# The first and third difference of W_v: a negation, an adding transfer and another order of subtraction

## The chip, the core and the metric

One core of a Trainium2 chip runs the kernel. TensorE multiplies into PSUM, VectorE (DVE), ScalarE (ACT) and GpSimd (POOL) work on SBUF, the first two of them on PSUM as well, and SyncE (SP), ScalarE and GpSimd issue transfers. The metric is the time of one execution in microseconds on the device, as the median of several runs.

## What is computed

A layer of masked attention over 2708 nodes of 1024 features, with a normalised input and a residual:

```python
h = relu(layernorm(x))
q = h @ W_q.T + b_q; k = h @ W_k.T + b_k; v = h @ W_v.T + b_v
z = (q @ k.T) / sqrt(1024) * adj
z = where(z == 0, -10000, z)
out = x + relu(softmax(z, axis=1) @ v)
```

`adj` is 2708 x 2708 with about 4 ones in a row (each is one with probability 0.0014771). Everything is float32.

## The kernel before

**Algebra.** The scores need only M = W_q^T W_k, formed once; then q = h M per tile of 128 nodes, and a score is the dot product of a node's row of q with a neighbour's row of h. The sums of neighbours are taken over rows of h, and W_v is applied to those sums. So the large products are h M ("q" units) and u W_v ("o" units), u being the weighted sums.

**Units.** A unit is two tiles against a 1024 x 1024 matrix B. It is done with seven block products of 512 x 512 instead of eight. B is needed as blocks B11, B21, B22 and as four differences: T0 = B12 - B11, T1 = B22 - T0, T2 = B22 - B12, T3 = B21 - T1. They live in two SBUF tensors: `M[:, i, j]` holds block Bij (8 KB a partition each), `T[:, 0..3]` the differences (`T` is a view of the tensor `wlow`). Ten q units (n = 0 to 9, B = M) are followed by ten o units (n = 10 to 19, B = W_v) and one single tile. `last_q` is 9. Block `M[:, 0, 1]`, B12, enters no product: it is used only to form T0 and T2.

**A unit's products, in TensorE's order** (`multiply`): s2 T1 into bank Y, a12 B21 into X, s4 B22 into Z, s3 T2 into Y; then, for the next unit already (`opened`), a11 B11 into its X, a ScalarE copy of X as its Y (`psy`, line 1024), s1 T0 into its Z, a copy of that as `p5` (line 1027); and last a22 T3 into this unit's Y. Between s3 T2 and a22 T3 the bank Y is read: in the last q units by VectorE's add of line 1092, in earlier or later ones through a ScalarE copy (`taken`, line 1076).

**Blocks of W_v** replace those of M as the last q unit finishes with each place. Lines 1263 to 1266 issue the five loads on SP's queue: B12 at step (n - last_q, i) = (-1, 0), the others at (0, 0) to (0, 4), and lines 1267 to 1270 the four subtractions on VectorE, 128 x 2048 elements each. `i` counts the places in a unit where other work is slipped in (`after(i)`).

**Gathers.** A neighbour's rows come by indirect transfers of 512 KB that GpSimd issues (line 610) into slots of 4 KB a partition; VectorE reads a slot for a score (line 863, with the tile's q rows, `pq`) and again for the weighted sum (line 923), then the slot is free for the next gather. There are 11 slots, and after step (1, 1) two more, cut from `M[:, 0, 1]`. Each transfer of GpSimd's queue also waits for the one eight places ahead of it to land.

**What sets the order.** VectorE's order is written by hand in the text of the program. From unit 4 on those of ScalarE, GpSimd, TensorE and SP are made by the scheduler of the language, which places an instruction when it expects its inputs to be ready; so a load or a ScalarE step may stand units ahead of the place where the text issues it.

Of the kernel before, what the change touches and what calls it, by code (L numbers as in the profile page):

```python
# [14 lines left out]
AF = mybir.ActivationFunctionType  # L15
ALU = mybir.AluOpType
# [49 lines left out]
def tile_preln_masked_attention(  # L66
# [12 lines left out]
    nc = tc.nc  # L79
# [3 lines left out]
    scale = 1.0 / math.sqrt(D)  # L83
# [116 lines left out]
    M = core.tile([P, 2, 2, 4, NB], FT, name="M")  # L200
# [232 lines left out]
    T = wlow.rearrange("p (k a) (b w) -> p k (a b) w", a=2, b=2)  # L433
# [12 lines left out]
    with tc.tile_pool(name="w", bufs=1, side="left") as wp:  # L446
# [11 lines left out]
        t1 = [work.tile([P, D], FT, tag="hT", name=f"t1_{k}", bufs=2) for k in range(2)]  # L458
# [61 lines left out]
        if True:  # L520
# [13 lines left out]
            for o in range(DC):  # L534
# [4 lines left out]
                else:  # L539
                    k = o - H  # L540
# [18 lines left out]
        Z = [psum.tile([P, NB], FT, tag="acc", name=f"ps_z{i}") for i in range(H)]  # L559
# [44 lines left out]
    def small(name):  # L604
        return half.tile([P, NB], FT, tag="half", name=name, bufs=14)
# [183 lines left out]
    slots, free = [], []  # L789
# [219 lines left out]
    def add_block(bank, a, b, last=True):  # L1009
        for c in range(4):  # L1010
            mm = nc.tensor.matmul(bank, a[:, c, :], b[:, c, :], start=False, stop=(c == 3), skip_group_check=True)  # L1011
        return mm
# [3 lines left out]
    def opened(n):  # L1016

        if n not in banks_of:
            return
        X, Z = banks_of[n]  # L1020
        ops = ops_of[n][0]
        add_block(X, ops["a11"], M[:, 0, 0])
        Y = psum.tile([P, NB], FT, tag="acc", name="psy")
        nc.scalar.copy(Y, X)
        products.append(add_block(Z, ops["s1"], T[:, 0]))
        p5 = small("p5")
        nc.scalar.copy(p5, Z)
        opened_of[n] = Y, p5

    def between(n):  # L1030

        if n == len(units) - 1:
            single["first"] = one_started(single["banks"], single["turned"][:, 0:4, :])
        else:
            opened(n + 1)
# [9 lines left out]
    def multiply(n, results, after):  # L1045


        X, Z = banks_of.pop(n)
        ops = ops_of.pop(n)[0]
        Y, p5 = opened_of.pop(n)  # L1050
        after(0)
        after(1)
        products.append(add_block(Y, ops["s2"], T[:, 1]))
        u2 = small("u2")
        nc.scalar.copy(u2, Y)
        after(2)
        add_block(X, ops["a12"], M[:, 1, 0])
        results[0](X)
        after(3)
        products.append(add_block(Z, ops["s4"], M[:, 1, 1]))  # L1060
        results[2](Z, u2)
        after(4)
        products.append(add_block(Y, ops["s3"], T[:, 2]))
        results[1](Y, p5)
        after(5)
        between(n)
        add_block(Y, ops["a22"], T[:, 3])
        results[3](Y)
        after(6)
# [117 lines left out]
    def of_wv(i, j):  # L1187

        return wv[j][:, i * 4:(i + 1) * 4, :]
# [5 lines left out]
    units = [("q",) + p for p in q_pairs] + [("o",) + p for p in o_pairs]  # L1195
# [19 lines left out]
    products = []  # L1215
    last_q = len(q_pairs) - 1
# [10 lines left out]
    single = {}  # L1227

    opened(0)
    for n, unit in enumerate(units):  # L1230
        kind, ta, tb = unit
# [12 lines left out]
        def after(i):  # L1244
# [13 lines left out]
            if n == FIRST and i in (1, 4, 5):  # L1258
                for g in slots[:4] if i == 1 else slots[4:6] if i == 4 else slots[6:8]:
                    with tc.issue_after(sorted_at[-1].ins):  # L1260
                        nc.vector.memset(g, 0.0)
            b11, b12, b21, b22 = M[:, 0, 0], M[:, 0, 1], M[:, 1, 0], M[:, 1, 1]
            for at, place, src in (((-1, 0), b12, of_wv(0, 1)), ((0, 0), b11, of_wv(0, 0)), ((0, 2), T[:, 1], of_wv(1, 1)),
                                   ((0, 3), b21, of_wv(1, 0)), ((0, 4), b22, of_wv(1, 1))):
                if (n - last_q, i) == at:
                    nc.sync.dma_start(place, src)
            for at, place, a, b in (((0, 2), T[:, 0], b12, b11), ((0, 4), T[:, 1], T[:, 1], T[:, 0]),
                                    ((1, 0), T[:, 2], b22, b12), ((1, 1), T[:, 3], b21, T[:, 1])):
                if (n - last_q, i) == at:
                    nc.vector.tensor_sub(place, a, b)  # L1270
            if (n - last_q, i) == (1, 1):
                free.extend(M.rearrange("p i j (a c) w -> p i j a (c w)", a=2)[:, 0, 1, a, :] for a in range(2))
            if (n, i) == (FIRST, 5):
                next(stream)
            if (n, i) == (FIRST, 6):
# [39 lines left out]
            if nxt is None and i == 1:  # L1315
                uT = work.tile([P, D], FT, tag="hT", name="T_alone", bufs=2).rearrange("p (c q) -> p c q", q=P)
# [53 lines left out]
    y = work.tile([P, D], FT, tag="q", name="y_alone", bufs=4)  # L1370
    send(gather(y, x, alone, SLOTS, P))
    uT, (X, Z), p1 = single["turned"], single["banks"], single["first"]
    add_block(Z, uT[:, 0:4, :], T[:, 0])
    add_block(Z, uT[:, 4:8, :], M[:, 1, 1])
    nc.vector.tensor_add(p1, Z, p1)
    nc.vector.scalar_tensor_tensor(y[:, hi], p1, 0.0, y[:, hi], op0=ALU.max, op1=ALU.add)
# [9 lines left out]
    with tc.If(some > 0):  # L1386
# [19 lines left out]
        with tc.tile_pool(name="big", bufs=1, side="right") as big, tc.tile_pool(  # L1406
# [25 lines left out]
            for t, (t0, n) in enumerate(tiles):  # L1432
                ht = gen.tile([P, D], FT, tag="ht", name="g_h")
                nc.sync.dma_start(ht[:n], h_dram[t0:t0 + n, :])
                for s in range(DC // 4):
                    pt = psum.tile([P, 4, P], FT, tag="tp", name="g_pt")
                    for c in range(4):
                        k = s * 4 + c
                        nc.tensor.transpose(pt[:, c, :n], ht[:n, k * P:(k + 1) * P], ident[:n, :n])
                    nc.vector.tensor_copy(hT[:, s * 4:(s + 1) * 4, t0:t0 + n], pt[:, :, :n])  # L1440
            with tc.For_i(0, NT) as i:
# [9 lines left out]
                q = gen.tile([P, D + 1], FT, tag="q", name="g_q")  # L1451
# [25 lines left out]
                for b0 in range(0, N, NB):  # L1477
                    w = min(NB, N - b0)
# [84 lines left out]
```

## Time and profile before

| | us |
|---|---|
| three runs | 639.73, 642.82, 648.21 |
| median | 642.82 |
| the profiled execution | 638.0 |
| its span, first to last instruction | 636.3 |

TensorE's granted clock is 0.995 in the mean. Busy shares by engine: PE 98%, DVE 83%, POOL 57%, ACT 45%; the DMA engines moved 180.11 MB, a mean of 283 GB/s. A timeline row reads: start, duration, engine, line, operation, output<-inputs, shape, count, and in brackets the idle time before it and what ended that. The rows of a group in the list of lines end with busy time, mean ns of one, and idle time before. For indirect transfers a row of POOL is the issue, not the transfer; the line "DMA to landing" has the times from issue to the last byte.

### The profile page before, as it was taken

The page shows a single profiled execution, that of the slowest core. Times are in us where ns is not written, and L with a number is a line of the kernel's source. Part 1 is how long each engine was busy: PE and PEld are TensorE (multiplying, and loading weights), DVE is VectorE, ACT ScalarE, POOL GpSimd, SP SyncE. Part 2 cuts the span into 40 slices and gives each one's busy share as a digit, 9 for nine tenths or more (in the row PEclk, how much of TensorE's full clock was granted, in tenths as well). Part 3 has the DMA queues.
Part 4 walks back from the last instruction along what each step waited for, and adds up shares of the span by engine and source line. Part 5 has one row for each costly group of instructions (what it writes and reads, how often), then busy time and mean ns, then how long its engine had stood idle before and what let it go on. Part 6 is the DMA issues. An engine that isn't in the chain of part 4 may idle for free.

```text
span 636.3 us, 6139 instructions
## 1 busy us (share of the span) xinstructions
PE 624.6 (98%) x1627; PEld 315.5 (50%) x1627; DVE 525.7 (83%) x1021; ACT 283.5 (45%) x421; POOL 361.8 (57%) x383
## 2 busy tenths in 40 slices
PE   9999999999999999999999999999999999999994
PEld 5777766444444544444444434444444444444441
DVE  5999889897995755997889999999999989898341
ACT  3539975859667533424341243443343333422300
POOL 2649960975868277563742563576566777632431
PEclk9999999999999999999999999999999999999997
DMA  8998897598696439986699998999999999893761
GB/s 339 407 372 310 334 351 298 199 342 328 246 382 221 170 113 334 326 299 196 194 289 323 297 412 216 311 318 324 351 378 321 334 299 295 242 289 95 210 217 40
DMA packets 62352, 180.11 MB, mean 283 GB/s; under 512 B 10039, under 2 KB 17031, under 8 KB 61672
## 3 DMA queue, kind: packets, MB, share of 16 engines
q0 software_dynamic: 25136, 78.41, 39.4%
q1 hardware_dynamic: 31242, 80.19, 35.8%
q10 hardware_dynamic: 5934, 21.06, 8.5%
q8 instruction: 15, 0.25, 0.2%
q14 instruction: 25, 0.20, 0.1%
HBM read 147.23 MB, written 42.31 MB: 298 GB/s over the span
## 4 chain that ended last, share of the span: by engine, by line
PE 85%; DVE 6%; issue 4%; DMA 3%; SPq 1%; POOL 0%; ACT 0%; POOLq 0%; DVEq 0%; ACTq 0%
PE ps L1011 38%; PE psy L1011 28%; PE ps_y L476 6%; PE ps_x L476 4%; PE ps_z L476 4%; PE pt L415 3%; DVE u L923 2%; DMA g<-h_dram,tab 1%; DMA or<-u_dram 1%; DVE junk L863 1%; DVE s L722 1%; DVE wlow L1270 1%; PE ps_y L511 1%; SPq L700 1%; DVE q L1092 0%
## 5 line engine op out<-in xcount | busy, mean ns | idle before, releaser
L610 POOL DMA_INDIRECT g<-h_dram,tab x94 | 121.4, 1291 | 84.4 <-DVE u L923 31.1
L1011 PE MATMUL ps<-M,a 128*128 128x512 f32 x320 | 144.0, 593 | 0.0
L1011 PE MATMUL psy<-wlow,s 128*128 128x512 f32 x320 | 143.9, 592 | 0.0
L863 DVE SCALAR_TENSOR_TENSOR junk<-g,pq 128x1024 uint8<-128x1024 f32 x93 | 113.7, 1222 | 14.0 <-DMA g<-h_dram,tab 10.9
L1011 PEld LDWEIGHTS ps<-M,a 128*128 128x128 f32 x320 | 59.8, 190 | 70.8 <-issue 70.6
L1011 PEld LDWEIGHTS psy<-wlow,s 128*128 128x128 f32 x320 | 59.7, 190 | 70.2 <-issue 69.4
L923 DVE SCALAR_TENSOR_TENSOR u<-g,coef,u 128x1024 f32<-128x1024 f32 x69 | 88.4, 1281 | 6.9 <-ACT u L912 5.8
L389 DVE FIND_INDEX8 at<-ones,adj 128x8 uint32<-128x685 f32 (+1 forms) x88 | 74.5, 865 | 0.0
L1011 PE MATMUL psy<-wlow,a 128*128 128x512 f32 x160 | 72.0, 593 | 1.4 <-DVE q L1092 1.4
L1011 PE MATMUL ps<-M,s 128*128 128x512 f32 x160 | 72.1, 592 | 0.0
L1011 PE MATMUL ps<-wlow,s 128*128 128x512 f32 x160 | 72.0, 593 | 0.1
L368 ACT ACTIVATE sized<-adj 128x2708 uint8<-128x2708 f32 (+1 forms) x22 | 54.3, 2468 | 7.5 <-DMA adj<-in_adj_dram 6.2
L298 POOL TENSOR_TENSOR hsum<-hsum,x 128x256 f32<-128x256 f32 (+1 forms) x56 | 38.7, 729 | 25.6 <-DVE wlow L444 21.2
L1110 POOL DMA_INDIRECT y<-in_x_dram,tab x19 | 34.8, 1832 | 29.1 <-ACT y L1127 15.9
L1011 PEld LDWEIGHTS psy<-wlow,a 128*128 128x128 f32 x160 | 30.3, 190 | 40.0 <-issue 37.1
L1011 PEld LDWEIGHTS ps<-wlow,s 128*128 128x128 f32 x160 | 30.3, 190 | 38.6 <-issue 37.9
L1011 PEld LDWEIGHTS ps<-M,s 128*128 128x128 f32 x160 | 30.3, 190 | 38.1 <-issue 37.4
L912 ACT ACTIVATE u<-g,coef 128x1024 f32<-128x1024 f32 x18 | 20.7, 1147 | 32.1 <-DVE coef L911 32.1
L808 POOL DMA_INDIRECT out_dram<-y,tab x21 | 25.0, 1188 | 16.4 <-DVE flag L1354 6.1
L626 POOL DMA_INDIRECT tab_dram<-tab,pos_i x22 | 21.9, 995 | 20.7 <-DVE pos_i L689 15.3
L276 ACT ACTIVATE x<-x,r 128x1024 f32<-128x1024 f32 (+1 forms) x22 | 25.9, 1235 | 7.3 <-POOL r L266 7.3
L760 ACT COPY ps<-bp_sb 128x512 f32<-128x512 f32 x42 | 24.5, 595 | 7.2 <-DVE y L1145 6.7
(251 smaller groups left out, 843.5 us busy)
## 6 DMA issues: line engine op xcount, KB each, us to landing
adj<-in_adj_dram SPq DMA_DIRECT2D x21, 1354.0 KB, 11.3
x<-in_x_dram SPq DMA_DIRECT2D x21, 512.0 KB, 3.9
h_dram<-x ACTq DMA_DIRECT2D x21, 512.0 KB, 8.7
u_dram<-v ACTq DMA_DIRECT2D x13, 512.0 KB, 6.4
or<-u_dram SPq DMA_DIRECT2D x52, 128.0 KB, 7.0
q_late<-q SPq DMA_DIRECT2D x12, 512.0 KB, 6.0
pq<-q_late SPq DMA_DIRECT2D x12, 512.0 KB, 8.6
M<-in_wv_dram SPq DMA_DIRECT2D x4, 1024.0 KB
```

The costliest lines, as they stand in the source:

```text
L276: nc.scalar.activation(xs[i][:n], xs[i][:n], AF.Relu, bias=r[:n, 4, i:i + 1], scale=r[:n, 3, i:i + 1])
L298: small.append(nc.gpsimd.tensor_add(hsum[:n, cols], hsum[:n, cols], xt[:n, cols]))
L368: nc.scalar.activation(sized[:n], a[:n, :, :PW], AF.Abs, accum_out=total[:n, t:t + 1])
L389: nc.vector.max_index(at[:n, k - first_k, g, :], ones[:n, 0:8], a[:n, g, :])
L476: mm = nc.tensor.matmul(bank, a_tile(o + H * a[0], a[1], i), b(o), start=first and o == 0, stop=(o == H - 1), skip_group_check=True)
L610: return nc.gpsimd.indirect_dma_start(out=dst, out_offset=None, in_=src, in_offset=off, bounds_check=N - 1, oob_is_err=False)
L760: nc.scalar.copy(return_[h], row[:, h * NB:(h + 1) * NB])
L808: to = nc.gpsimd.indirect_dma_start(out=out, out_offset=bass.IndirectOffsetOnAxis(ap=ptab.bitcast(U32)[:n, t, SLOTS:SLOTS + 1], axis=0), i ...
L863: chained(lambda: nc.vector.scalar_tensor_tensor(junk, g_of[t][s], 1.0, tq[t], op0=ALU.mult, op1=ALU.mult, accum_out=zall[:, t, s:s + 1]))
L923: chained(lambda: nc.vector.scalar_tensor_tensor(u, g_of[t][s], coef[:, s:s + 1], u, op0=ALU.mult, op1=ALU.add))
L1011: mm = nc.tensor.matmul(bank, a[:, c, :], b[:, c, :], start=False, stop=(c == 3), skip_group_check=True)
L1110: return nc.gpsimd.indirect_dma_start(out=y[:n], out_offset=None, in_=x, in_offset=off, compute_op=ALU.add)
```

## The change

W_v's blocks and differences are formed otherwise:

- Block B11 is loaded into `M[:, 0, 1]` (issued in the text at step (-2, 0)), ScalarE negates it in place in two halves, and an adding transfer on GpSimd's queue adds B12 to it from DRAM. What was T0 then stands in `M[:, 0, 1]` (called `t1`).
- The subtraction for T0 on VectorE falls away. T2 is formed as T1 - B11 instead of B22 - B12, which is the same.
- The o units and the single tile read the first difference from `M[:, 0, 1]`; the q units go on reading T0 from `T[:, 0]`.
- The two further gather slots are cut from `T[:, 0]` instead of `M[:, 0, 1]`, and are given at step (0, 0) instead of (1, 1).

```diff
-        products.append(add_block(Z, ops["s1"], T[:, 0]))
+        products.append(add_block(Z, ops["s1"], T[:, 0] if units[n][0] == "q" else M[:, 0, 1]))
...
-            b11, b12, b21, b22 = M[:, 0, 0], M[:, 0, 1], M[:, 1, 0], M[:, 1, 1]
-            for at, place, src in (((-1, 0), b12, of_wv(0, 1)), ((0, 0), b11, of_wv(0, 0)), ((0, 2), T[:, 1], of_wv(1, 1)),
+            b11, t1, b21, b22 = M[:, 0, 0], M[:, 0, 1], M[:, 1, 0], M[:, 1, 1]
+            for at, place, src in (((-2, 0), t1, of_wv(0, 0)), ((0, 0), b11, of_wv(0, 0)), ((0, 2), T[:, 1], of_wv(1, 1)),
                                    ((0, 3), b21, of_wv(1, 0)), ((0, 4), b22, of_wv(1, 1))):
                 if (n - last_q, i) == at:
                     nc.sync.dma_start(place, src)
-            for at, place, a, b in (((0, 2), T[:, 0], b12, b11), ((0, 4), T[:, 1], T[:, 1], T[:, 0]),
-                                    ((1, 0), T[:, 2], b22, b12), ((1, 1), T[:, 3], b21, T[:, 1])):
+            if (n - last_q, i) == (-2, 6):
+                for h in range(2):
+                    nc.scalar.activation(t1[:, 2 * h:2 * h + 2], t1[:, 2 * h:2 * h + 2], AF.Copy, scale=-1.0)
+                nc.gpsimd.dma_start(t1, of_wv(0, 1), accum_op=ALU.add)
+            for at, place, a, b in (((0, 4), T[:, 1], T[:, 1], t1), ((1, 0), T[:, 2], T[:, 1], b11),
+                                    ((1, 1), T[:, 3], b21, T[:, 1])):
                 if (n - last_q, i) == at:
                     nc.vector.tensor_sub(place, a, b)
-            if (n - last_q, i) == (1, 1):
-                free.extend(M.rearrange("p i j (a c) w -> p i j a (c w)", a=2)[:, 0, 1, a, :] for a in range(2))
+            if (n - last_q, i) == (0, 0):
+                free.extend(T.rearrange("p k (a c) w -> p k a (c w)", a=2)[:, 0, a, :] for a in range(2))
...
-    add_block(Z, uT[:, 0:4, :], T[:, 0])
+    add_block(Z, uT[:, 0:4, :], M[:, 0, 1])
```

On ScalarE, in unit 4, behind the last copies that prepare its banks (line 760; the rows of line 379 and before are squares of M, of which two read `M[:, 0, 1]`), the difference of the two orders is:

```order
 L379 ACTIVATE junk_b,msq<-bp_sb 128x1024
 L760 COPY ps_1591<-bp_sb 128x512
+L1269 ACTIVATE M<-M 128x1024 x2
 L1076 COPY taken<-psy 128x512
 L1024 COPY psy<-ps_1589 128x512
```

The negations stand five units ahead of the last q unit, directly ahead of the copies of lines 1076 and 1024. The load into `M[:, 0, 1]` keeps its place in SP's queue.

On GpSimd, in unit 5, between the gathers of a tile (`g`, from h) and the rows of a later unit (`qr`):

```order
 L610 DMA g_1412<-h_dram,tab 128x1024
 L610 DMA g_1413<-h_dram,tab 128x1024
+L1270 DMA M<-in_wv_dram 128x2048
 L612 DMA qr_1737<-h_dram,tab 128x1024
 L612 DMA qr_1739<-h_dram,tab 128x1024
```

The adding transfer is one more transfer of that queue; what stood behind it stands one place later.

On ScalarE at the end of unit 10, the first with W_v, before:

```order
L1076 COPY taken<-psy 128x512
L1027 COPY p_2550<-ps_2497 128x512
L945 COPY v_2505<-u_2444 128x8x4x32
L1127 ACTIVATE y_2406<-u_2440 128x512
L947 DMA u_dram<-v_2505 128x1024
L1024 COPY psy<-ps_2495 128x512
L1134 ACTIVATE y_2407<-psy 128x512
```

and of the changed kernel:

```order
L1076 COPY taken<-psy 128x512
L945 COPY v_2507<-u_2446 128x8x4x32
L1127 ACTIVATE y_2408<-u_2442 128x512
L947 DMA u_dram<-v_2507 128x1024
L1024 COPY psy<-ps_2497 128x512
L1027 COPY p_2552<-ps_2499 128x512
L1123 ACTIVATE y_2409<-p_2380 128x512
```

The copy of line 945 (a finished weighted sum, put into another order for its store) now precedes both bank copies of the next unit, lines 1024 and 1027. TensorE's order differs in one place, the same turn: before, half of unit 11's product s4 B22 stood ahead of its s2 T1; now s2 T1 follows a22 T3 directly and s4 B22 is undivided. VectorE's order is the same but for the subtraction that is gone and the slots that are read.

## The prediction

> **What bounds the kernel now.** I read the page's busy times first, then the waits of TensorE, then its timeline where it waited, then VectorE's timeline before that wait.
>
> ```profile
> PE 624.6 (98%) x1627; PEld 315.5 (50%) x1627; DVE 525.7 (83%) x1021; ACT 283.5 (45%) x421; POOL 361.8 (57%) x383
> ```
>
> TensorE is busy for 624.6 of 636.3 us: 11.7 us is all that is not already matmul, beginning and end included. Asked what TensorE waited for in the middle, the view of waits has one answer:
>
> ```profile
> PE psy L1011 <- DVE q L1092: 1.4, 1, 1.4
> ```
>
> Its timeline there (start, duration, 8 records = one product of four 128x512 blocks):
>
> ```profile
> 360.38 3.60 PE L1011 MATMUL ps<-M,a 128*128 128x512 f32 x8
> 363.81 3.60 PE L1011 MATMUL ps<-wlow,s 128*128 128x512 f32 x8
> 368.81 3.70 PE L1011 MATMUL psy<-wlow,a 128*128 128x512 f32 x8 [1.41 <-DVE q L1092]
> 372.35 3.60 PE L1011 MATMUL psy<-wlow,s 128*128 128x512 f32 x8
> ...
> 386.08 3.60 PE L1011 MATMUL ps<-M,a 128*128 128x512 f32 x8
> 389.74 3.67 PE L1011 MATMUL ps<-wlow,s 128*128 128x512 f32 x8
> ...
> 396.68 1.88 PE L1011 MATMUL ps<-M,s 128*128 128x512 f32 x4
> ```
>
> Undisturbed, products start 363.81 - 360.38 = 3.43 us apart, so start to start is the honest measure: durations overlap. Ten products lie between the first and the last row, so 396.68 - 360.38 - 10 x 3.43 = 2.0 us are lost: 368.81 - 363.81 - 3.43 = 1.57 at the wait, 0.11 behind it, 389.74 - 386.08 - 3.43 = 0.23 at the next unit's s1, the rest in crumbs. All lies in the turn from W_q products to W_v products. Next, who was late there:
>
> ```profile
> 352.79 2.28 DVE L1270 TENSOR_TENSOR wlow<-M 128x2048 f32<-128x2048 f32 x1
> ...
> 363.37 2.28 DVE L1270 TENSOR_TENSOR wlow<-wlow 128x2048 f32<-128x2048 f32 x1
> ...
> 368.08 0.68 DVE L1092 TENSOR_TENSOR q<-psy,p 128x512 f32<-128x512 f32 x1
> ...
> 388.90 0.69 DVE L722 TENSOR_TENSOR s<-a,s 128x512 f32<-128x512 f32 x1
> ```
>
> The first row is the difference that the change takes away (T0). VectorE has no wait between these rows up to the add of line 1092, which ends at 368.08 + 0.68 = 368.76, and the product starts at 368.81: it waits for that add. Likewise s1 (line 722) ends at 389.59 and its product starts at 389.74. VectorE is late, TensorE pays.
>
> The Trainium skill (Perfetto Trace Analysis, Identifying the Most-Contended Engine) calls matmul busy time a bad measure of distance to the limit, and weight-load busy a good one, 50% here; by it there would be room in TensorE. The even 3.43 us says that this program's stream leaves no gap, and the change alters no product.
>
> **Removed: T0 = B12 - B11 on VectorE.** One instruction of 2.28 us. All that stands behind it on VectorE starts up to 2.28 us earlier: the add then ends at 366.48, before the product could start at 363.81 + 3.43 = 367.24 (margin 0.76). s1 would end at 387.31 and its product wants to start at 389.51 - 1.57 - 0.11 = 387.83 (margin 0.37 after the 0.15 from end to start). So the losses go: -2.0 us. The margin of 0.37 is also the price list: of any new delay of VectorE, what exceeds 0.37 us comes back nearly one for one, and at about 2.3 us the gain is nothing.
>
> **Added: load, two negations on ScalarE.** T2 = T1 - B11 instead of B22 - B12 is the same size: zero. The first load stands where the old one stood in SP's queue, with the same bytes.
>
> ```profile
> 219.26 0.33 SPq L1266 DMA_DIRECT2D M<-in_wv_dram  x1
> ```
>
> The transfer view of 218 to 227 us (40 slices of 0.225 us):
>
> ```profile
> DMA  9994200007981986569999975300200000300001
> GB/s 437 382 437 164 73 0 0 0 0 182 255 182 36 328 218 255 218 291 473 400 400 473 439 307 213 91 21 0 39 3 0 0 0 0 41 0 0 0 0 18
> ```
>
> The block moves from the 10th to the 26th slice, so it has landed at about 224 us. ScalarE, around the place where the negations now stand, with the nearest price (128x1024, float32 to float32) and TensorE's next write to the bank that the copy behind them reads:
>
> ```profile
> 226.76 0.62 ACT L760 COPY ps<-bp_sb 128x512 f32<-128x512 f32 x1
> 231.69 0.59 ACT L1076 COPY taken<-psy 128x512 f32<-128x512 f32 x1 [4.31 <-PE psy L1011]
> L912 ACT ACTIVATE u<-g,coef 128x1024 f32<-128x1024 f32 x18 | 20.7, 1147 | 32.1 <-DVE coef L911 32.1
> 238.35 3.60 PE L1011 MATMUL psy<-wlow,a 128*128 128x512 f32 x8
> ```
>
> 2 x 1.147 = 2.3 us, from 227.4 to 229.7, inside 4.31 us of idleness: zero. Were the load as late as 233 us, the copies queued behind would still be done before 238.35.
>
> **Added: the adding transfer, 1 MB in GpSimd's queue.** Its place is between the last gather of one tile and two row loads:
>
> ```profile
> 251.92 1.29 POOL L612 DMA_INDIRECT qr<-h_dram,tab  x1 [0.30 <-issue]
> 257.94 0.94 POOL L612 DMA_INDIRECT pq<-q_dram,tab  x1 [3.46 <-DVE junk L863]
> 261.16 1.01 POOL L610 DMA_INDIRECT g<-h_dram,tab  x1 [0.30 <-issue]
> 271.07 1.22 DVE L863 SCALAR_TENSOR_TENSOR junk<-g,pq 128x1024 uint8<-128x1024 f32 x1
> 272.33 1.25 DVE L863 SCALAR_TENSOR_TENSOR junk<-g,pq 128x1024 uint8<-128x1024 f32 x1
> 267.57 1.04 PE L415 MATMUL pt<-ident,qr 128*128 128x128 f32 x8
> ```
>
> Issue: no row shows an adding load with whole rows, so the bounds are the plain one (line 845) and the slowest adding gather (line 1110):
>
> ```profile
> L845 POOL DMA_DIRECT2D g<-v_dram x2: 573/592/612, 344.2 to 558.7; - x2
> L1110 POOL DMA_INDIRECT y<-in_x_dram,tab x19: 1571/1635/2628, 397.1 to 600.6; - x19
> DMA to landing us min/median/max: 6.2/10.1/14.4
> ```
>
> 0.6 to 2.6 us, taken 1.6, the median of the kind that adds. Up to 3.46 of it is hidden by GpSimd's wait ahead of 257.94. VectorE can stretch an issue:
>
> ```profile
> 380.11 2.25 DVE L1270 TENSOR_TENSOR wlow<-M,wlow 128x2048 f32<-128x2048 f32 x1
> 380.23 3.00 POOL L610 DMA_INDIRECT g<-h_dram,tab  x1 [0.30 <-DVE a L705]
> ```
>
> Beside that difference of two SBUF operands a gather took 3.00 us instead of 1.01; even so it is hidden. The Trainium skill (SBUF — State Buffer, Who interferes with whom) reports that such a tensor_tensor did not stall DMA in its probe; by that the issue would cost only its own 0.6 to 2.6. These two rows differ from it.
>
> Bytes: the DMA engines are nearly full there:
>
> ```profile
> 250.00:272.00 22.00, 22.00 (x60) 10.18 (x59) 19.24 (x34) 9.24 (x15) 13.00 (x12) 1.00 0.93 337
> ```
>
> 1.05 MB at 337 GB/s is 3.1 us more for whoever is behind. The gather of 261.16 is read at 272.33, the key rows of 257.94 from 271.07. Gathers land so after issue:
>
> ```profile
> DMA to landing us min/median/max: 2.4/7.9/14.5
> ```
>
> 261.16 + 7.9 = 269.1, a slack of 3.3 us against 3.1: I take zero, bounds zero and a delay worked out below. A gain is excluded: it only adds bytes. The row loads at 251.92 are turned by TensorE only at 267.57.
>
> **Moved: two slots, ScalarE's order.** Two gathers now stand right behind line 845 (344.2 us), not behind the third W_v difference. VectorE's waits from 298 to 452 us, first and last of five groups:
>
> ```profile
> DVE u L923 <- ACT u L912: 3.0, 2, 1.6
> ...
> DVE w L886 <- ACT w L872: 0.3, 1, 0.3
> ```
>
> All five name ScalarE, none a gather: gathers that land earlier gain nothing there, and their 1 MB only moves. On ScalarE a copy of line 945, which waits for VectorE, now stands ahead of the bank copies of lines 1024 and 1027 behind unit 10, and TensorE lost the half product that it did there ahead of time:
>
> ```profile
> 391.56 2.60 DVE L923 SCALAR_TENSOR_TENSOR u<-g,coef,u 128x1024 f32<-128x1024 f32 x2
> 394.19 1.05 ACT L945 COPY v<-u 128x1024 f32<-128x1024 f32 x1 [0.16 <-DVE u L923]
> 395.68 0.58 ACT L1024 COPY psy<-ps 128x512 f32<-128x512 f32 x1
> ```
>
> With VectorE 2.28 earlier, line 945 starts at 391.9 and line 1024 ends 396.26 - 394.19 = 2.07 later, 394.0; the product that needs it wants 396.68 - 2.0 = 394.7. Margin 0.7: zero, bound 1.5 if VectorE is not earlier. The end:
>
> ```profile
> 606.89 0.59 ACT L760 COPY ps<-bp_sb 128x512 f32<-128x512 f32 x1 [6.71 <-DVE y L1145]
> 609.69 3.60 PE L1011 MATMUL ps<-M,T_alone 128*128 128x512 f32 x8
> ```
>
> The last banks are ready 2.2 us ahead, so the end moves along by 2.0. Sum: 638.0 - 2.0 = 636.0 us for an execution like the profiled one (636.3 span + 1.7 around it). The three runs' median, 642.82, lies 4.8 above it; so 642.8 - 2.0 = 640.8.
>
> **Rivals.** *The adding transfer is late (slower).* For it: it heads GpSimd's queue, and its work per byte may be more; two adding gathers of 512 KB at the slowest, 2 x 14.4 = 28.8 us, would land it at 280.7, the key rows behind it no sooner, 9.6 us after 271.07. VectorE has little room afterwards, so TensorE pays 9.6 - 2.3 = 7.3: 645.3 as profiled, 650 as median. It decides from a landing past 271 us, 19 after issue; 2% needs 15 us late. Against it: two medians, 20.2 us, put it at 272.1, 1.1 us late and nearly free. The Trainium skill (DMA: Bandwidth & Descriptors, Measured) gives 6.15 us for a plain 1 MB load from GpSimd: by this estimate it would be done by 260. *Nothing gained:* the gap only changes its name, because VectorE's later waits use up 2.28; 642.8. *ScalarE's new order costs up to 1.5:* 642.3; for it the 0.7 margin. *More gained:* if the runs' 4.8 us over the profile are the same lateness of VectorE, all of it may go: 638.0 less the 2.0 at the most, 636.
>
> **Numbers.** Forecast 0.50, nothing gained 0.17, new order 0.10, late transfer 0.15 (0.05 of it past 2%), more gained 0.08. The forecast's own spread is that of the runs, 639.73 to 648.21. Range 636 to 648: from more gained to most of the late transfer. 2% (12.9 us) is about what a measurement here tells from no change; faster by that needs more than the 11.7 us TensorE does not use: 0.02. Slower 0.05, within 0.93.
>
> **What will show it.** Right: no wait of TensorE on line 1092; products 3.43 apart from 360 to 400; four differences become three; VectorE's add ends near 366.5. The negations sit in an idle stretch near 228. Wrong: VectorE waiting for a gather or key rows near 271, TensorE waiting for ScalarE near 395, or a wait at 387 in place of the one at 368.

## The result and the profile after

| | before | after |
|---|---|---|
| runs | 22 | 22 |
| median, us | 641.14 | 645.22 |
| lowest to highest | 639.73 to 648.21 | 640.2 to 649.21 |
| profiled execution's span | 636.3 | 645.5 |

The ratio of after to before is 1.0051, with a 95% interval of 1.0032 to 1.0071: some 3 us slower, where 2.0 us of gain were forecast. The runs of after fall into two groups of eleven: 640.2 to 644.4 us at a granted clock of 0.992 to 0.996, and 646.1 to 649.2 at 0.988 to 0.993. The profiled one is of the upper group, which the expectations below call the slow group; one run of 648.86 us in run 16 counts in no ratio.

The page's line of busy times, after:

```profile
PE 629.4 (98%) x1627; PEld 317.7 (49%) x1627; DVE 523.6 (81%) x1020; ACT 287.0 (44%) x423; POOL 358.5 (56%) x384
```

VectorE does 2.1 us less, TensorE is busy 4.8 us longer with the same 1627 records: some of them ran slower. The view of TensorE's waits has another answer than before:

```profile
PE ps L1011 <- DVE s L722: 3.0, 1, 3.0
PE pt L415 <- DMA qr<-h_dram,tab: 2.8, 1, 2.8
PE ps_y L511 <- POOL hsum L121: 1.2, 1, 1.2
```

The wait of 1.4 us for line 1092 is gone. The second row lies near 200 us, ahead of all that the change touches; with the clock at 0.83 from 200 to 210 it puts TensorE 4.9 us behind the earlier profile by 220 us. It is no part of the change: the profiles of runs 13 to 16, all from one chip, show it at 1.6 to 2.8 us, and run 15 among them is the kernel before with an added transfer (1.8); the profiles of runs 1 to 12, from two other chips, don't show it. The first row is the change's. TensorE's timeline of after around it (as before: 8 records are one product):

```profile
365.25 3.60 PE L1011 MATMUL ps<-M,a 128*128 128x512 f32 x8
368.68 3.60 PE L1011 MATMUL ps<-M,s 128*128 128x512 f32 x8
372.11 3.60 PE L1011 MATMUL psy<-wlow,a 128*128 128x512 f32 x8
...
389.28 3.60 PE L1011 MATMUL ps<-M,a 128*128 128x512 f32 x8
395.88 6.64 PE L1011 MATMUL ps<-M,s 128*128 128x512 f32 x8 [3.01 <-DVE s L722]
402.36 1.88 PE L1011 MATMUL psy<-wlow,a 128*128 128x512 f32 x4
```

The product that waited at 368.81 before (`psy<-wlow,a`, here at 372.11) comes 3.43 us behind its forerunner: nothing lost. At the next unit's s1, 395.88 - 389.28 - 3.43 = 3.17 us are lost to a wait, and then 402.36 - 395.88 - 3.43 = 3.05 more while s1 itself runs. The windows view says why (columns: stretch, length, busy time and records of TensorE, weight load, VectorE, ScalarE, GpSimd, then granted clock, DMA share, GB/s):

```profile
392.00:394.00 2.00, 0.88 (x3) 0.05 (x1) 1.93 (x7) 1.31 (x3) 0.00 (x0) 1.00 0.00 0
394.00:396.00 2.00, 0.12 (x1) 0.15 (x1) 1.93 (x4) 0.51 (x2) 0.00 (x0) 0.76 0.35 111
396.00:398.00 2.00, 2.00 (x3) 0.96 (x4) 1.97 (x4) 0.00 (x0) 0.00 (x0) 0.50 1.08 272
...
402.00:404.00 2.00, 2.00 (x6) 0.88 (x5) 1.97 (x7) 1.02 (x3) 1.70 (x2) 1.00 0.92 201
```

Behind the wait the granted clock is half, for 6 us: a wait of 3.0 us costs 6.2 in all. The 4.9 near 200 and these 6.2, less the 2.0 gained at 368, make 9.1 of the 9.2 us between the two profiled spans. VectorE, in front of s1, and SP's queue, in order of time:

```profile
368.75 7.93 SPq L1085 DMA_DIRECT2D q_late<-q  x2
376.79 17.35 SPq L833 DMA_DIRECT2D pq<-q_late  x3
381.07 2.25 DVE L1274 TENSOR_TENSOR wlow<-M,wlow 128x2048 f32<-128x2048 f32 x1
388.41 1.23 DVE L863 SCALAR_TENSOR_TENSOR junk<-wlow,pq 128x1024 uint8<-128x1024 f32 x1 [5.09 <-DMA pq<-q_late]
395.05 0.69 DVE L722 TENSOR_TENSOR s<-a,s 128x512 f32<-128x512 f32 x1
```

VectorE comes to the score of tile 17 at 383.3 and waits 5.1 us for that tile's q rows (`pq`). The load (line 833) is issued at 376.79, behind the stores of q tiles 18 and 19 (line 1085), of which the second waits for ScalarE's copy of the last q product. So its issue goes with TensorE, and not with VectorE, which is now early. Meanwhile the DMA engines are taken as full; the stretch from 352 us in after, then in before:

```profile
352.00:388.00 36.00, 36.00 (x86) 15.91 (x85) 28.74 (x41) 11.39 (x19) 15.23 (x10) 1.00 1.02 348
```

```profile
352.00:384.00 32.00, 30.59 (x72) 13.28 (x71) 30.79 (x40) 8.52 (x14) 20.20 (x12) 1.00 1.04 359
```

The shares are 1.02 and 1.04: in the mean over the 16 engines, the packets' times add up to more than the stretch. Before, the load was issued at 373.84, and VectorE came to these rows at 382.29 and found them there:

```profile
373.84 14.16 SPq L833 DMA_DIRECT2D pq<-q_late  x3
382.29 1.22 DVE L863 SCALAR_TENSOR_TENSOR junk<-g,pq 128x1024 uint8<-128x1024 f32 x1
```

How long they had been there can be read from SP's queue, which waits for the same load further on. The last semaphore wait of line 833 ends with the landing; in before, then in after:

```profile
L833 SPq EVENT_SEMAPHORE  x5: 17/27/3587, 373.8 to 378.2; - x5
L833 SPq EVENT_SEMAPHORE  x5: 17/28/5904, 376.7 to 382.4; - x5
```

In after that is 382.4 + 5.9 = 388.3, and VectorE, which was waiting, starts 0.1 us later. In before it is 378.2 + 3.6 = 381.8: the rows were there 382.29 - 381.8 - 0.1 = 0.4 us before VectorE came.

### The profile page after: what moved, and what is told of

It is laid out like the page before. It is cut to its first block, busy times and chain, and to the rows that moved or that the text cites. A ratio compares the mean times of both kernels' runs of the same rounds, so it can differ in the third digit from the quotient of the medians.

```text
span 645.5 us, 6146 instructions
## 1 busy us (share of the span) xinstructions
PE 629.4 (98%) x1627; PEld 317.7 (49%) x1627; DVE 523.6 (81%) x1020; ACT 287.0 (44%) x423; POOL 358.5 (56%) x384
## 4 chain that ended last, share of the span: by engine, by line
PE 94%; DMA 3%; DVE 1%; issue 0%; POOL 0%; ACT 0%; POOLq 0%; SPq 0%; DVEq 0%; ACTq 0%
PE ps L1011 43%; PE psy L1011 31%; PE ps_y L476 6%; PE ps_x L476 4%; PE ps_z L476 4%; PE pt L415 4%; DMA pq<-q_late 2%; DMA qr<-h_dram,tab 1%; PE ps_y L511 1%; DVE junk L863 0%; PE ps_h L1223 0%; PE ps_v L594 0%; DVE s L722 0%; DVE y_alone L1383 0%; POOL out_dram L1367 0%
## 5 line engine op out<-in xcount | busy, mean ns | idle before, releaser
L610 POOL DMA_INDIRECT g<-h_dram,tab x94 | 117.8, 1253 | 89.4 <-DVE u L923 44.1
L1011 PE MATMUL ps<-M,s 128*128 128x512 f32 x240 | 110.9, 606 | 3.0 <-DVE s L722 3.0
L923 DVE SCALAR_TENSOR_TENSOR u<-g,coef,u 128x1024 f32<-128x1024 f32 x70 | 89.7, 1281 | 7.3 <-ACT u L912 6.0
L1011 PEld LDWEIGHTS ps<-M,s 128*128 128x128 f32 x240 | 46.5, 195 | 62.2 <-issue 61.7
L1110 POOL DMA_INDIRECT y<-in_x_dram,tab x19 | 33.2, 1745 | 32.8 <-ACT y L1127 15.9
L1011 PE MATMUL ps<-wlow,s 128*128 128x512 f32 x80 | 36.0, 592 | 0.0
L476 PE MATMUL ps_y<-wlow 128*128 128x512 f32 x64 | 27.6, 592 | 0.0
```

The costliest lines, as they stand in the source:

```text
L476: mm = nc.tensor.matmul(bank, a_tile(o + H * a[0], a[1], i), b(o), start=first and o == 0, stop=(o == H - 1), skip_group_check=True)
L610: return nc.gpsimd.indirect_dma_start(out=dst, out_offset=None, in_=src, in_offset=off, bounds_check=N - 1, oob_is_err=False)
L923: chained(lambda: nc.vector.scalar_tensor_tensor(u, g_of[t][s], coef[:, s:s + 1], u, op0=ALU.mult, op1=ALU.add))
L1110: return nc.gpsimd.indirect_dma_start(out=y[:n], out_offset=None, in_=x, in_offset=off, compute_op=ALU.add)
```

## The experiments

Sixteen runs, each beside the kernel before on its chip. The letters of the theories: A, the load of q tile 17 is late for a VectorE that is early; B, the negations and the adding transfer cost the time; C, the two gathers that moved ahead crowd the DMA engines; D, the scheduler's new orders; the others are named where they come up. The measured numbers in one table; "beyond" counts the runs more than 1 us longer than the longest of the kernel before in the same comparison.

| run | kernel | ratio to before | beyond | VectorE's wait for the load | TensorE's at s1 |
|---|---|---|---|---|---|
| 1 | after, stores by ScalarE | 0.9986 [0.9977, 0.9994] | 0 of 11 | 1.68 | 0.27 |
| 2 | after, slots given later | 1.003 [1.001, 1.005] | 3 of 12 | 3.28 | 1.18 |
| 3 | after, slots later, idle subtraction | 1.0017 [1.0009, 1.0026] | 0 of 12 | 1.04, put down to a gather | 1.19 |
| 4 | after without negations, adding transfer | 1.0066 [1.0042, 1.0089] | 7 of 9 | 6.25 | 4.57 |
| 5 | after again | 1.0046 [1.0017, 1.0075] | 5 of 9 | 2.89 | 0.81 |
| 6 | before, stores by ScalarE | 0.9991 [0.998, 1.0001] | 0 of 12 | none | none |
| 7 | after, B22 later | 1.0045 [1.0021, 1.0068] | 7 of 12 | none | none |
| 8 | after, B22 later, stores by ScalarE | 1.0038 [1.0011, 1.0066] | 6 of 12 | none | none |
| 9 | after, two gathers held back | 1.0005 [0.9994, 1.0016] | 0 of 11 | 2.77 | 1.54 |
| 10 | after, VectorE held back | 0.9999 [0.999, 1.0008] | 0 of 11 | 0.29 | 0.44 |
| 11 | after, gathers held back, stores by ScalarE | 0.9972 [0.9961, 0.9983] | 0 of 7 | none | none |
| 12 | before, VectorE 3.7 us later | 1.0083 [1.0069, 1.0097] | 5 of 5 | none | 3.94 |
| 13 | after, 1 MB less traffic | 0.9981 [0.996, 1.0001] | 0 of 10 | none | none |
| 14 | after, 1 MB more traffic | 1.0128 [1.0105, 1.0151] | 4 of 4 | 8.41 | 6.33 |
| 15 | before, 1 MB more traffic | 1.0059 [1.0034, 1.0084] | 2 of 7 | 3.33 | 3.48 |
| 16 | after again | 1.0043 [1.0011, 1.0076] | 5 of 10 | 3.38 | 1.29 |

**1. The stores out of the load's way.**

```diff
-            (nc.scalar if t < 4 else nc.sync).dma_start(dst, q)
+            (nc.scalar if t < 4 or t >= BARE - 2 else nc.sync).dma_start(dst, q)
```

> The changed kernel, with the stores of the last two q tiles (18 and 19) issued by ScalarE, which makes their last half, and no longer by SyncE. Theory A (the load of q tile 17's rows stands in SyncE's queue behind these two stores, so it cannot start before TensorE has ended the last q unit, and VectorE, now early, waits 5.1 us for it just ahead of s1): the load starts near 366, some 10 us earlier than at 376.8, VectorE's wait for it goes, and with it TensorE's 3.0 us at 395.9 and the low clock behind it; the median is 638.5 to 641.5, that is 3.5 to 6 below the changed kernel's 645.2. Theory B (the negations and the adding transfer cost the time) and theory C (the two slots given earlier crowd the DMA engines and stretch the load to 11.5 us): 644 to 646, with VectorE still waiting for that load or for others. Theory D (the scheduler's new order of ScalarE and TensorE costs the time): 644 to 646, with other waits of TensorE.

The load starts at 366.28 and TensorE's wait is 0.27 us, no run falls into an upper group, the kernel is faster than before. But the load issued 6 us earlier than in its neighbours still lands only at 381.38. SP's and VectorE's rows:

```profile
366.28 20.83 SPq L833 DMA_DIRECT2D pq<-q_late  x3
381.38 1.23 DVE L863 SCALAR_TENSOR_TENSOR junk<-wlow,pq 128x1024 uint8<-128x1024 f32 x1 [1.68 <-DMA pq<-q_late]
```

It takes 15 us for 512 KB: the place behind the two stores is not all that holds it up. That the rest is traffic is argued from the DMA share above 1; runs 9 to 16 test it.

**2. Slots given later.**

```diff
-            if (n - last_q, i) == (0, 0):
+            if (n - last_q, i) == (1, 1):
                 free.extend(T.rearrange("p k (a c) w -> p k a (c w)", a=2)[:, 0, a, :] for a in range(2))
```

> The changed kernel, with the two extra gather slots given at step (1,1) of the first o units as before, instead of (0,0). Theory C (the two gathers moved earlier crowd the DMA engines): the load of q tile 17 lands in 8.5 us in place of 11.5, VectorE's wait falls from 5.1 to about 2, TensorE's 3.0 us stall goes, median 640 to 642. Theory A: the load starts where it did (behind the two stores, near 376.8), and VectorE arrives as early as before, so a wait of 3 to 5 us and a stall of 1 to 3 us of TensorE stay, median 643 to 646. Theories B and D: 644 to 646.

This did not do what it was made for: the scheduler put the two gathers where the block comes free all the same, at 342.71 and 344.43. So the choice of the block moved them, not the step. For the stretch in question the run is the changed kernel once more, and says nothing on theory C.

**3. An idle subtraction on VectorE.** Slots as in run 2, and:

```diff
-            for at, place, a, b in (((0, 4), T[:, 1], T[:, 1], t1), ((1, 0), T[:, 2], T[:, 1], b11),
+            for at, place, a, b in (((0, 2), T[:, 0], t1, b11), ((0, 4), T[:, 1], T[:, 1], t1), ((1, 0), T[:, 2], T[:, 1], b11),
```

> The changed kernel with slots at (1,1) as before and with a subtraction of 128x2048 put back on VectorE at its old place (its result is read by nobody), so that VectorE is as late as in the kernel before while the negations and the adding transfer stay. Theory A: VectorE's wait for q tile 17 falls by the 2.28 us of the subtraction below that of the run without it, TensorE's stall at 395 goes or is under 1 us, its wait near 368 for the sum on VectorE comes back (about 1.5 us); median 640.5 to 642.5, as before the change. Theory B: 644 to 646, since what it blames is still there. Theory D: 644 to 646.

No run falls into an upper group, as theory A has it and B and D don't. VectorE's wait ahead of tile 17 falls from run 2's 3.28 to 1.04 us, by the length of the subtraction; the view puts the 1.04 down to a gather, but the load's last completion mark in the trace stands 0.13 us before VectorE starts, so the two came together. Two things were missed: s1 still waits 1.19 us, and TensorE's wait near 368 did not come back (0.15 us lost). And the run does more than it was meant to: the subtraction writes the block of the two slots, so their gathers went out at 355.34 and 357.92, some 12 us later than in run 2. It holds back both causes that runs 9 and 10 take apart.

**4. Without the negations and the adding transfer.**

```diff
-            if (n - last_q, i) == (-2, 6):
-                for h in range(2):
-                    nc.scalar.activation(t1[:, 2 * h:2 * h + 2], t1[:, 2 * h:2 * h + 2], AF.Copy, scale=-1.0)
-                nc.gpsimd.dma_start(t1, of_wv(0, 1), accum_op=ALU.add)
```

> The changed kernel without the two negations on ScalarE and without the adding transfer on GpSimd: the block holds plain B11, so W_v's differences are formed from the wrong block and this part of the computation is left out; all later instructions are there. Theory B: 640.5 to 642, as before the change. Theory A: VectorE arrives as early as in the changed kernel, the load of q tile 17 starts where it did, and the stall at 395 stays; 644 to 646.

The upper group stays, and TensorE waits 4.57 us: theory B falls.

**5. The changed kernel beside the others.**

> The changed kernel once more, beside the others on one chip. Theory A (the load of q tile 17 comes too late for a VectorE that is earlier): TensorE's wait at s1 of the second o unit, 3.0 us in the first profile, is there again (2.5 to 5 us, and the granted clock at half for some us behind it), since the variant with the slots as before had 1.2 us and the one without the adding transfer 4.6 us; VectorE waits 4 to 6.5 us for that load; ratio to before 1.004 to 1.009. Theory F (the 645.5 us of the first profile came from the wait of 2.8 us near 200, which stands in code that the change does not touch, and the wait at s1 is an accident of that run): no wait near 200 here, a wait at s1 under 1.5 us, ratio 0.997 to 1.002.

Two groups again, 636.9 to 638.3 us at a granted clock of 0.995 or 0.996 and 642.3 to 643.9 at 0.990 to 0.993; the profile happened on the lower one, with 0.81 us of TensorE's wait. Its ratio and its groups are as theory A says, its profile is not: the landing changes from run to run. Theory F falls: no profile of this chip has the wait near 200, those of longer runs (643.07 in run 7, 645.17 in run 12) included.

**6. The stores alone, on the kernel before** (run 1's edit).

> The kernel before, with the stores of q tiles 18 and 19 issued by ScalarE. A control for the run with that edit on the changed kernel: in the kernel before VectorE comes to the rows of q tile 17 at 382.3 and doesn't wait for them, so an earlier load gives nothing. Theory A: the load starts near 366 in place of 373.8, TensorE's waits of 1.4 us near 368 and 0.2 us at s1 stay, ratio to before 0.998 to 1.001. If the two stores on SyncE cost something by themselves, whatever VectorE does, this run is faster by about as much as the changed kernel became (0.5% or more, ratio under 0.996).

The load, issued at 360.95 and not near 366, is not waited for, and the wait at 368 is 0.76 us where the profile of before had 1.41. No gain that can be told from none: where VectorE is late, the stores cost nothing that shows.

**7 and 8. The load ahead of B22's**, in run 8 with run 1's edit as well.

```diff
-                                   ((0, 3), b21, of_wv(1, 0)), ((0, 4), b22, of_wv(1, 1))):
+                                   ((0, 3), b21, of_wv(1, 0)), ((1, 1), b22, of_wv(1, 1))):
```

> The changed kernel, with the load of B22 at step (1,1) of the first o units in place of (0,4): the third difference is no longer formed from B22, which is first read by a product near 402. In SyncE's queue the load of q tile 17 then stands ahead of B22's 1 MB and of the store of q tile 19, behind B21's load and the store of q tile 18 alone. Theory E (the DMA engines are full from 352 to 385 us in all of these kernels, and the load lands when what was queued ahead of it has gone: with the two stores on ScalarE it was issued 6 us earlier and still landed only near 381): the load lands before 379, VectorE does not wait for it, TensorE's wait at s1 goes (under 0.4 us), ratio to before 0.996 to 0.999. Theory A in its first form (only the place behind the two stores counts, not the traffic): also gone, since the load is ahead of one of them, but with a wait of VectorE left where the traffic does nothing. Against both: B22 late, with a wait of TensorE near 402.

> Both edits on the changed kernel: B22's load at (1,1), and the stores of q tiles 18 and 19 issued by ScalarE. Theory E: the load of q tile 17 is issued right behind B21's, near 361 to 366, with 1 MB less ahead of it than in the run with the stores alone, so it lands by 377 in place of 381; no wait of VectorE for it, none of TensorE at s1; what is left is what VectorE's own work sets, ratio to before 0.996 to 0.998, as much as the first reckoning promised (2 us) or less.

VectorE's wait went, as expected, with the load issued at 365.58 and read at 378.63. But the expectation had the wrong product for B22's first use: it is s4 of the first o unit, near 378, not one near 402. TensorE, run 7:

```profile
374.10 3.60 PE L1011 MATMUL ps<-M,a 128*128 128x512 f32 x8
381.56 6.52 PE L1011 MATMUL ps<-M,s 128*128 128x512 f32 x8 [3.86 <-DMA M<-in_wv_dram]
387.91 3.60 PE L1011 MATMUL psy<-wlow,s 128*128 128x512 f32 x8
```

Whichever of the two loads is last comes late; that the two gathers ahead of both are why is not shown here. B22 is late by 3.86 us here and by 2.30 in run 8.

**9 and 10. One of the two causes at a time.** Run 9 holds the two gathers back (VectorE stays early), run 10 holds VectorE back (the gathers stay early).

```diff
+            if (n - last_q, i) == (1, 0):
+                nc.vector.memset(T[:, 0, 0, 0:1], 0.0)
+                nc.vector.memset(T[:, 0, 2, 0:1], 0.0)
-            if (n - last_q, i) == (0, 0):
+            if (n - last_q, i) == (1, 1):
                 free.extend(T.rearrange("p k (a c) w -> p k a (c w)", a=2)[:, 0, a, :] for a in range(2))
```

```diff
+            if (n - last_q, i) == (0, 2):
+                for _ in range(2):
+                    junk = work.tile([P, D], mybir.dt.uint8, tag="junk", name="junk3", bufs=1)
+                    nc.vector.scalar_tensor_tensor(junk, bp_sb, 1.0, bp_sb, op0=ALU.mult, op1=ALU.mult)
```

> The changed kernel with the two extra slots given at (1,1), and held back there: VectorE writes one column of each behind the second difference (0.06 us apiece), so that the first two gathers into them wait for it, as they did in the kernel before (near 375, and not near 343; giving the slots later alone did not move these two gathers). The subtraction stays away, so VectorE stays 2.28 us early. Theory C' (the DMA engines are full from 352 to 385, and the two gathers, 1 MB or about 2.5 us at the 415 GB/s of that stretch, have moved ahead of the load of q tile 17): the load lands near 379.5 in place of 382 to 385, VectorE waits for it 1 us at most, TensorE's wait at s1 is under 0.4 us, no run falls 4 us behind the rest with the lower clock, ratio to before 0.997 to 1.000. Theory A' (only VectorE's earliness counts, the traffic ahead is the same): VectorE waits 2 to 5 us for the load as in the changed kernel, ratio 1.002 to 1.006, a part of the runs at 641 and above.

> The other half: the changed kernel, gathers early as it has them, with two products of bp_sb into the junk tile added on VectorE where the subtraction stood (2 x 1.2 us, read by nobody), so that VectorE is as late as before. Theory C': the load still lands at 382 to 385, VectorE comes to it near 382, so it waits 0 to 3 us, and some runs still fall into the slow group at 641 and above; ratio 1.002 to 1.005. Theory A': VectorE's wait falls by 2.4 us against the changed kernel, to 0 to 1, TensorE's wait at s1 to 0 to 0.5 with the wait near 368 back, no run in the slow group, ratio 0.999 to 1.002.

Either one empties the upper group, so it takes both. Run 10 is as theory A' said: wait at s1 0.44, the wait near 368 back with 1.13. Run 9 is C' in its times and A' in its profile: VectorE still waited 2.77 us, and the load landed at 382.17, no earlier than the 381.95 of run 5. How the gathers work is therefore shown by the times alone.

**11. Both remedies**: the edits of runs 9 and 1 together.

> Both remedies on the changed kernel: the two gathers held back as before, and the stores of q tiles 18 and 19 issued by ScalarE. By theory C' as by A', the load of q tile 17 is issued near 366 with 1 MB less ahead of it and lands by 379; VectorE does not wait for it, TensorE's wait at s1 goes (the run with the stores alone had 0.3 us), and the whole of the gain promised at 368 is left: ratio to before 0.997 to 0.9985, the fastest of all.

The lowest ratio of all, 1.8 us below before (0.0028 x 638.1; 1.1 to 2.5 by the interval, 1.5 by the medians), and steady: 636.18 to 636.83. The stores' own share, 0.0009 in run 6 and not told from none, is in it. SP's, VectorE's and TensorE's rows, and the windows view:

```profile
362.08 22.53 SPq L833 DMA_DIRECT2D pq<-q_late  x3
378.90 1.21 DVE L863 SCALAR_TENSOR_TENSOR junk<-g,pq 128x1024 uint8<-128x1024 f32 x1
384.92 3.60 PE L1011 MATMUL ps<-M,a 128*128 128x512 f32 x8
388.35 3.60 PE L1011 MATMUL ps<-M,s 128*128 128x512 f32 x8
391.78 3.60 PE L1011 MATMUL psy<-wlow,a 128*128 128x512 f32 x8
```

```profile
352.00:384.00 32.00, 32.00 (x76) 14.12 (x75) 30.42 (x50) 9.74 (x17) 17.69 (x12) 1.00 1.02 357
```

TensorE is busy for all 32 us, at s1 too: 3.43 between starts.

**12. The price of a wait, on the kernel before.** Three of run 10's products at step (1, 1).

> The price of a wait of TensorE by itself, on the kernel before: three products of bp_sb into the junk tile (3 x 1.2 us, read by nobody) added on VectorE just ahead of its work for s1 of the second o unit. The prediction's reckoning (what exceeds 0.37 us of a new delay comes back nearly one for one): TensorE waits 3.2 to 3.5 us at 389 and the kernel is 3.2 to 3.5 us longer, ratio 1.005. Theory G (a wait of TensorE of over some 2 us lowers the granted clock to half for the next 6 us, and costs about 3 us more): the same wait, the clock at 0.5 behind it, 6 to 7 us longer, ratio 1.0095 to 1.011.

```profile
386.23 3.60 PE L1011 MATMUL ps<-M,a 128*128 128x512 f32 x8
393.76 6.58 PE L1011 MATMUL ps<-wlow,s 128*128 128x512 f32 x8 [3.94 <-DVE s L722]
400.18 3.60 PE L1011 MATMUL psy<-wlow,a 128*128 128x512 f32 x8
```

4.10 us lost to the wait, 400.18 - 393.76 - 3.43 = 2.99 behind it, as theory G said; the times, 5.3 us above before, are a little under its 6 to 7 and well over the 3.4 of one for one.

**13 to 16. The traffic ahead of the load.** Run 13 drops the load of B22; its absence also lets the scheduler put the load of tile 17 ahead of the store of q tile 19:

```diff
-                                   ((0, 3), b21, of_wv(1, 0)), ((0, 4), b22, of_wv(1, 1))):
+                                   ((0, 3), b21, of_wv(1, 0))):
```

Runs 14 and 15 add 1 MB, run 16 is the changed kernel as it is:

```diff
+            if (n - last_q, i) == (0, 5):
+                nc.sync.dma_start(m_dram[1, 1], T[:, 1])
```

> The changed kernel without the load of B22 (1 MB; products and rows that need that block are left out in effect, since it holds old weights). Theory T (the load of q tile 17 lands when what is queued ahead of it in the full DMA engines has gone): 1 MB at 415 GB/s less, so it lands 2 to 3 us earlier than in the changed kernel, near 379 to 380; VectorE waits 1 us at most for it, TensorE's wait at s1 is gone, no run with a lowered clock; ratio to before 0.997 to 0.999. Theory I (its landing is set by when it is issued, behind the store of q tile 18, and by its own run time): lands as before, ratio 1.002 to 1.006.

> The changed kernel with 1 MB of DMA more: SyncE stores the first sum of the o units' block to a spare place in DRAM right behind the load of B22, at 361 to 366, read by nobody. Theory T: the load of q tile 17 lands 2 to 3 us later, near 384.5; VectorE waits 5 to 6 us in every run, TensorE 3 to 4 at s1 with the clock at half behind it; nearly all runs in the slow group, ratio to before 1.008 to 1.011. Theory I: as the changed kernel, ratio 1.002 to 1.006.

> The same 1 MB more on the kernel before. Theory T: the load lands near 384, where VectorE, which comes at 382, waits 1 to 3 us for it and TensorE 1 to 3 at s1; a part of the runs falls into a slow group that the kernel before has never shown in over 80 runs; ratio 1.001 to 1.007. If instead the kernel before is as fast as ever (0.999 to 1.001), its load lands well ahead of VectorE, and what makes the changed kernel's load late is more than VectorE's 2.28 us and the two gathers.

> The changed kernel once more, as the reference for the runs with 1 MB less and 1 MB more, on their chip. The two looks at it so far gave a wait of VectorE of 5.1 and 2.9 us and of TensorE of 3.0 and 0.8: a landing that changes from run to run by some 2 us, and two groups of times 4 to 5 us apart. Expected: median 1.003 to 1.006 of before, both groups seen, and the profile's group goes with its wait: TensorE's wait under 1.6 us and a clock of 0.995 or more, or over 2.2 us and 0.993 or less.

VectorE's row of run 14, then of run 16:

```profile
389.17 1.23 DVE L863 SCALAR_TENSOR_TENSOR junk<-wlow,pq 128x1024 uint8<-128x1024 f32 x1 [8.41 <-DMA pq<-q_late]
```

```profile
384.23 1.23 DVE L863 SCALAR_TENSOR_TENSOR junk<-wlow,pq 128x1024 uint8<-128x1024 f32 x1 [3.38 <-DMA pq<-q_late]
```

With the load issued within 0.1 us of the same moment (374.23 and 374.32), 1 MB more ahead of it makes it land 4.9 us later: twice the 2.5 us reckoned from 415 GB/s, but theory T and not I. In the kernel before the same 1 MB brings the same wait: its load was not far ahead of VectorE either. That is one profile of each, and landings spread (below); that all four of run 14's times lie beyond bears it out. Run 13 lost the wait, though for two reasons at once. The profile of run 16 is one of the lower group, with the wait that belongs to it. A low clock does not always come from s1, though: run 13's profile has none of that wait, and 0.993 all the same, with 2.77 us of wait near 200 and the clock at 0.83 from 200 to 210. On this chip the kernel before, too, has five runs of 641.81 to 643.31 us at 0.992 to 0.994; "beyond" counts from above these.

## Why the prediction was wrong

**The gain at 368 came.** The add of line 1092 no longer makes TensorE wait, in any profile of the unaltered changed kernel; with nothing in the way (run 11) some 1.8 us of the promised 2.0 are there. But 2.0 was the loss of one profile: in those of runs 6, 12 and 15, where VectorE does the same work up to that add, the wait at 368 is 0.76, 0.73 and 0.20 us in place of 1.41. The negations take 2.03 us and lie in ScalarE's idle time; the adding transfer's issue takes 1.04 us (the sum took 1.6), its 1 MB lands 12.5 us after issue (run 5), and GpSimd waits 2.89 us behind it where it had 3.46. Of the rivals, the late adding transfer and ScalarE's new order are refuted, the first by run 4, the second by there being no wait of TensorE on ScalarE in after. "More gained" is as well: with both remedies it is 1.8 us.

**The step that failed** is "All that stands behind it on VectorE starts up to 2.28 us earlier", carried on to s1 with a "margin of 0.37": it takes for granted that VectorE up to s1 needs only its own work. The waits between 298 and 452 us, "All five name ScalarE, none a gather", seemed to bear it out, and were read rightly. But a wait that isn't there says nothing about how near it is. Just ahead of s1 VectorE reads a load that SP issues, not GpSimd; its margin was not looked at, and it was 0.4 us against the 2.28 that VectorE gained.

Take the start of VectorE's read, which the landing releases, against the start of TensorE's product a11 ahead of s1. In all ten profiles that put a wait of VectorE down to this load, TensorE's wait at s1 is that difference plus 3.88 us, to within 0.02; eight of them:

| | run 1 | run 5 | run 9 | run 16 | after | run 15 | run 4 | run 14 |
|---|---|---|---|---|---|---|---|---|
| landing less start of a11, us | -3.61 | -3.07 | -2.33 | -2.58 | -0.87 | -0.39 | 0.70 | 2.45 |
| TensorE's wait at s1, us | 0.27 | 0.81 | 1.54 | 1.29 | 3.01 | 3.48 | 4.57 | 6.33 |

So once VectorE waits there, s1 comes when the load comes, and what VectorE saved before is worth nothing. In the kernel before VectorE itself stood at 382.29 - 386.08 = -3.79: the wait of 1.57 us at 368 holds TensorE back while the transfers go on, and the rows were there. An estimate from these rows: without the 1.57 and the 0.11 behind it, a11 would start at 384.40, and a load that lands as it did, read from 381.9 on, makes s1 wait 381.9 - 384.40 + 3.88 = 1.4 us. That would leave some 0.6 of the 2.0 us, with nothing else changed. With that wait back in run 10, the read stood at -3.43 and the upper group was gone. The change took the wait away and the load's lateness came to light.

**"Gathers that land earlier gain nothing"** was priced at zero and had the wrong sign: in a stretch whose DMA share is above 1, two gathers moved ahead put 1 MB ahead of the load. Held back (run 9) the upper group is gone, though the load of that run's profile landed no earlier.

**"One for one"** failed as well. A wait of 1.54 us or less at s1 cost nothing beyond itself but 0.08 us; one of 3 us or more cost 2.9 to 3.05 more through the clock, in run 15 1.8.

**The rival "nothing gained"**, whose gap only changes its name, was right in kind, and a wait at 387 was named as the sign of it; it was given 0.17 and priced at no change. It holds for the lower group of runs. What it lacked is a longer wait and the clock behind it: the upper group is 4 to 5 us slower, of which, going by the profiles, some 3 are the clock's and the rest the wait's.

Open: why the landing differs from run to run (by 2.2 us against a11 over the three profiles of the changed kernel), so that half of the runs fall into each group; whether the gathers' 1 MB acts through that spread, as run 9's times say, when its one landing was no earlier; and why 1 MB cost 4.9 us in run 14.

## What to carry to other kernels

Ask of each engine that becomes earlier not only what it waits for now, but what it reads next and when that arrived: a transfer that was read without a wait may have landed just in time, above all where the windows view shows the DMA engines full. Work that is freed to start earlier there can move ahead of what is urgent, so look whether the order of the transfers has to be changed with it. And price a wait of TensorE by its length: in these profiles a new one of up to 2.06 us cost itself and some 0.1 us more, and each of 2.30 us and over brought the half clock.

## What was not expected of the hardware

The granted clock answers waits in steps. Lost behind the wait at s1 (in runs 7 and 8 at s4), worked out from starts as above: 0.08 us after waits of 0.81, 1.18, 1.29 and 1.54 us; 1.8 after 2.30 (run 8) and 3.48 (run 15); 2.9 to 3.05 after 3.01, 3.86 (run 7), 3.94, 4.57 and 6.33. The clock falls to 0.5 in these windows, not lower, and a longer wait makes it no worse. The waits near 200 draw the same line: behind 1.55, 1.80 and 2.06 us (runs 14, 15 and 16) the clock stays at 1.00, behind 2.76 and 2.77 (after and run 13) it falls to 0.5. The windows view behind the wait of run 15 (3.48 us, s1 starts at 394.34), then of run 12 (3.94 us, s1 starts at 393.76):

```profile
394.00:396.00 2.00, 1.66 (x3) 0.72 (x4) 1.93 (x4) 0.00 (x0) 0.00 (x0) 0.84 0.99 295
396.00:398.00 2.00, 2.00 (x4) 0.94 (x3) 1.96 (x3) 0.00 (x0) 0.29 (x1) 0.50 1.13 171
398.00:400.00 2.00, 2.00 (x5) 0.77 (x5) 2.00 (x3) 0.25 (x1) 1.70 (x2) 0.80 1.15 213
400.00:402.00 2.00, 2.00 (x6) 0.93 (x5) 1.97 (x5) 2.00 (x4) 1.36 (x1) 1.00 1.11 195
```

```profile
394.00:396.00 2.00, 2.00 (x3) 0.91 (x4) 1.97 (x4) 0.00 (x0) 0.00 (x0) 0.50 1.10 257
396.00:398.00 2.00, 2.00 (x3) 0.67 (x2) 1.96 (x2) 0.00 (x0) 0.86 (x1) 0.50 1.15 213
398.00:400.00 2.00, 2.00 (x4) 0.86 (x3) 1.97 (x5) 1.78 (x3) 1.70 (x2) 0.60 1.16 192
400.00:402.00 2.00, 2.00 (x6) 0.87 (x5) 1.97 (x6) 1.02 (x3) 1.70 (x2) 1.00 0.71 197
```

Behind the wait the clock is low for some 3.6 us in run 15 (1.8 us lost at half) and for 6 in run 12; the waits differ by 0.5.

The Trainium skill (TensorE: Matmul & The Clock Gate, Part 1) says that the clock is halved after an idle window of about 3.4 us that runs free of the kernel, and comes back after about as long a busy one. Half clock, and a penalty that depends on how the wait lies in a window, agree with these rows (1.8 after 3.48 us, 3.05 after 3.01). That it takes 3.4 us of idleness does not: 2.30 and 3.01 us were enough. The low clock lasted 3.6 us behind the former and 6 behind the latter.
